# Macaron layer with an S4D mixing: float32 products of the output layer in one group of four banks per batch, and of the kernel's taps for four steps at a time

## The chip, the cores and the metric

One Trainium2 chip; the program runs on one of its cores. The metric is the device time of one execution in microseconds (us), as a median over runs. The engines are named as in the profile: PE (TensorE, the matrix products; PEld are its weight loads), DVE (VectorE), ACT (ScalarE), POOL (GpSimd), SP (the queue that issues most of the transfers).

## The reference, cut to what matters

B = 4 batches of L = 1024 tokens, D = 256 channels, HID = 1024, all float32:

```python
def ffn(x, w1, s1, w2, s2, h1, t1, h2, t2, w3, s3):
    h = silu((x @ w1.T) * s1) * ((x @ w2.T) * s2)     # 256 -> 1024
    h = gelu((h @ h1.T) * t1)                         # 1024 -> 1024
    h = gelu((h @ h2.T) * t2)                         # 1024 -> 1024
    return (h @ w3.T) * s3                            # 1024 -> 256

def mixing(x, ...):                                   # S4D
    K = 2 * einsum('dn,dnl->dl', C, exp(dtA[:, :, None] * t)).real   # taps, [D, L]
    y = irfft(rfft(x.T, 2 * L) * rfft(K, 2 * L), 2 * L)[:, :, :L]
    return gelu(y.T) @ W.T + b                        # W: the output layer, 256 -> 256

x = x + 0.5 * ffn(layernorm(x), ...)
x = x + mixing(layernorm(x), ...)
return x + 0.5 * ffn(layernorm(x), ...)
```

The matrices w1, w2, h1, h2 and w3 hold only -1, 0 and 1. The second `ffn` uses the same weights as the first.

## The kernel before, in words

**The FFN blocks.** The 4096 tokens are eight blocks of 512. The first FFN runs over f0 to f7, the second over g0 to g7. f0 to f7, g0 and g1 are single blocks (`ffn`, L374); g2 to g7 are three pairs of blocks whose two 1024 x 1024 layers use a Winograd scheme with 7 products in place of 8 (`ffn_pair`, L416). In a single block, `linear` (L362, matmuls at L366) makes one output tile of 128 x 512 in one PSUM bank: for each 128 rows of input a product with the high part of the activation and one with its low part, in a reduced float32 format that the profile calls fp32r. ACT applies the activation and copies the high part (`g`, L399; `h_f`, L401), DVE makes the low part by subtraction (`low_part`, L309). The products of w1 and w2 are `pa` and `pb`, those of h1 and h2 `p2` and `p3` (both are `p_f` or `p_g` in the profile, which leaves numbers out), those of w3 `po` (L617).

**The mixing.** It is an FFT convolution cut into matrix products, and these take true float32 operands; each such matmul is two records in the trace. Four kinds of them: `pk` (L883) makes the taps from the modes, once for the whole program; `pf` (L956) is the forward transform of the taps (`pf_k`) and of each batch (`pf_m`); `pi` (L1134) is the inverse transform; `pw` (L1159) is the output layer. All the rest of the mixing, complex products with `kr` and `ki` and butterflies (`y`, `z`, `p`, `q`, `u`, `v`, `w`), is element work on DVE through one helper (L155).

**How the two are laid together.** The mixing is written as generators. `all_aside` (L1221) runs the taps (`kernel_steps`), their transform (`kernel_spectrum`), then `mix(b)` for the four batches, each as soon as its two f blocks are done. In an `ffn` block, each of the 16 output tiles of h1 and h2 calls `tick` (L1245) after its own work has been written out, and `tick` advances the generator until an allowance of DVE work is used up (`STEP_WORK` 3600, 3400 once f7 is done; only operations on DVE count, not matmuls or ACT's copies) or until the generator yields `PAUSE`. So a `PAUSE` puts at least one output tile of FFN products between what is ahead of it and what is behind it. After a `PAUSE` with allowance left, in the later blocks, up to two steps of fillers may run: sums of weights for the pairs (`weight_sums`, stored to DRAM) and a check of the weights (`weight_checks`). `ahead` (L1279) moves the preparation of the next block on: load, norm, squares and a turn through DRAM (`sq`, `moved`, `xf`) and the split into parts (`parted`: `xt`, L356 and L309). A scheduler then fixes the order of each engine's list; each engine takes its list in order.

**Taps.** `kernel_steps` runs over two groups of channels; the first falls into block f1, the second into f2. In each, eight steps make a tile `p` on DVE (three operations, with `po`) and append it to `ready`. `products` makes eight `pk` matmuls from one step, 128 x 64 weights and 32 columns; two steps fill a bank, and eight ACT copies (L895, 64 x 64) then take that bank to the `taps` tiles.

**Output layer.** In `mix`, the inverse's result goes through the gelu to `yt`. Then, for j in steps of two, `xr` (128 x 512, part of x1) is loaded by SP, a bank `pw` takes four matmuls from `yt` and `wt_sb`, DVE adds the bias (`yw`), POOL adds `xr` (L1175), and a store to x2 (L1176) follows.

**Buffers.** All banks of PSUM, eight of 128 x 512, are one ring (`ps`). `half` (L167) is one ring of 19 tiles of 128 x 512 in SBUF, for nearly everything of the mixing and for `g`; `ring` (L171) is one of 15 for the activations in two parts. A tile of a ring waits for the last user of the tile that had its place before.

Of the kernel before, what the change touches and what calls it, by code (L numbers as in the profile page):

```python
# [21 lines left out]
J = L // P  # L22
# [86 lines left out]
def macaron_layers(  # L109
# [54 lines left out]
    def bank(name):  # L164
        return psum.tile([P, 512], F32, tag="ps", name=name)

    def half(name, *shape, dtype=F32):  # L167

        return work.tile([P, *(shape or (512,))], dtype, tag="half", name=name, bufs=19)
# [35 lines left out]
    def column(i):  # L205
        return cst_sb[:, i : i + 1]

    def positions(t, b, j, n=2):
        return t[b].rearrange("(p j) d -> p j d", j=J)[:, j : j + n, :]
# [599 lines left out]
    def powers(d0, first, n, name):  # L809


        ch = 512 // n
        at = cst_sb[:, None, first : first + n].to_broadcast([P, ch, n])

        def of(i):
            return adt[:, i, d0 : d0 + ch, None].to_broadcast([P, ch, n])

        a, k, e = (half(f"{t}_{name}", ch, n) for t in ("a", "k", "e"))
        tt(e, of(0), at, ALU.mult)
        nc.scalar.activation(e, e, AF.Exp)  # L820
        tt(a, of(1), at, ALU.mult)
        reduce_angle(a, a, k)
        yield
        c = k
        sin_cos(c, a)
        yield
        tt(c, c, e, ALU.mult)
        tt(a, a, e, ALU.mult)
        yield c, a
# [3 lines left out]
    def kernel_steps():  # L833


        yield from kernel_factors()
        taps.extend(half(f"taps_{i}", 2, 2, DD) for i in range(J // 2))
        n = 512 // NA
        group = 512 // A1
        shape = [P, n, A1, A0]  # L840
        for g0 in range(0, DD, group):

            for got in powers(g0, C_A1, A1, f"1_{g0}"):
                yield
            c, i = got
            to_re, to_im = half(f"to_re_{g0}", group, A1), half(f"to_im_{g0}", group, A1)
            ts(to_re, c, column(C_RE), None, ALU.mult)
            stt(to_re, i, column(C_IM), to_re, ALU.mult, ALU.add)
            ts(to_im, c, column(C_IM), None, ALU.mult)
            stt(to_im, i, column(C_MINUS_RE), to_im, ALU.mult, ALU.add)  # L850
            yield
            for fine in powers(g0, C_A0, A0, f"0_{g0}"):
                yield

            qd = []
            some = 512 // NB
            for d0 in range(g0, g0 + group, some):
                for got in powers(d0, C_B, NB, f"b_{d0}"):
                    yield
                c, i = got  # L860
                for t, m in ((c, 0), (i, 1)):
                    by = c_dt[:, m, d0 : d0 + some, None].to_broadcast([P, some, NB])
                    tt(t, t, by, ALU.mult)
                for d1 in range(0, some, per_tile):
                    t = half(f"qd_{d0 + d1}", per_tile, 2, NB)
                    nc.gpsimd.memset(t, 0.0)
                    qd.append(t)
                    for h in range(2):
                        part, ch = slice(h * 64, (h + 1) * 64), slice(d1, d1 + per_tile)
                        tt(t[part, :, h, :], c[part, ch], i[part, ch], ALU.add)  # L870
                yield

            pk = None
            ready = []

            def products(d1, a):

                nonlocal pk
                at = d1 % per_tile
                if at == 0:  # L880
                    pk = psum.tile([P, per_tile, 2, NB], F32, tag="ps", name=f"pk_{g0 + d1}")
                for i in range(n):
                    nc.tensor.matmul(  # L883
                        pk[0:NA, at + i, :, :].rearrange("p h b -> p (h b)"),
                        a[:, i].rearrange("p a b -> p (a b)"),
                        qd[d1 // per_tile][:, at + i, :, :].rearrange("p h b -> p (h b)"),
                        start=True,
                        stop=True,
                    )
                if at + n == per_tile:  # L890
                    first = g0 + d1 + n - per_tile
                    for i, t in enumerate(taps):
                        for over in range(NB // J):
                            b0 = over * J + 2 * i
                            nc.scalar.copy(  # L895
                                t[over * NA : (over + 1) * NA, :, :, first : first + per_tile],
                                pk[0:NA, :, :, b0 : b0 + 2].rearrange("p d h b -> p b h d"),
                            )

            for d1 in range(0, group, n):  # L900
                re, im = fine

                def outer(coarse, t):
                    return (
                        coarse[:, d1 : d1 + n, :, None].to_broadcast(shape),
                        t[:, d1 : d1 + n, None, :].to_broadcast(shape),
                    )

                a, o = (half(f"{t}_{g0 + d1}", n, A1, A0) for t in ("p", "po"))
                tt(a, *outer(to_re, re), ALU.mult)  # L910
                tt(o, *outer(to_im, im), ALU.mult)
                tt(a, a, o, ALU.add)
                ready.append((d1, a))
                if len(ready) == 4:
                    for old in ready[0:2]:
                        products(*old)
                    del ready[0:2]
                yield
            yield PAUSE
            for old in ready:  # L920
                products(*old)
            yield
# [113 lines left out]
    def mix(b, xn):  # L1036
# [108 lines left out]
        todo = []  # L1145
        for j in range(0, J, 2):
            xr = half(f"xr_{b}_{j}", 2, D)
            nc.sync.dma_start(xr, positions(x1, b, j))
            todo.append((j, xr))
            if len(todo) == 1:  # L1150
                continue
            yield PAUSE
            results = []
            for j, xr in todo:
                ps = bank(f"pw_{b}_{j}")
                results.append(ps)
                for e in range(2):
                    for dc in range(DC):
                        nc.tensor.matmul(  # L1159
                            ps[:, e * D : (e + 1) * D],  # L1160
                            yts[dc][j // JQ][:, (j % JQ + e) * P : (j % JQ + e + 1) * P],
                            wt_sb[:, dc, :],
                            start=(dc == 0),
                            stop=(dc == DC - 1),
                        )
            yield PAUSE
            for (j, xr), ps in zip(todo, results):
                y = half(f"yw_{b}_{j}", 2, D)
                tt(
                    y,  # L1170
                    ps.rearrange("p (e d) -> p e d", e=2),
                    bias_sb[:, None, :].to_broadcast([P, 2, D]),
                    ALU.add,
                )
                nc.gpsimd.tensor_tensor(y, xr, y, ALU.add)  # L1175
                stores.dma_start(positions(x2, b, j), y)  # L1176
            todo = []
# [43 lines left out]
    def all_aside():  # L1221


        yield from kernel_steps()
        yield from kernel_spectrum()
        xn = None
        for b in range(B):
            while ("f", 2 * b + 1) not in done:
                yield PAUSE
            if xn is None:  # L1230
                xn = [load_half(x1, b, g) for g in range(2)]
                yield PAUSE
            yield from mix(b, xn)
            xn = None
            done.append(("m", b))
# [150 lines left out]
```

## Time and profile before

| | before |
|---|---|
| median of 3 runs | 1368.81 us (1368.12 to 1369.08) |
| profiled execution, its own time | 1368.22 us |
| span from its first to its last instruction | 1366.4 us |
| clock granted to PE, mean | 0.999 of full speed |
| PE busy with matmuls / weight loads | 1351.8 us (99%) / 1125.2 us (82%) |
| DVE, ACT, POOL busy | 74%, 57%, 22% |
| `pk` (taps): 256 records | 16.4 us busy, 223 ns each, from 111.9 to 225.7 us |
| `pw` (output layer): 128 records | 28.9 us busy, 379 ns each, from 403.0 to 900.7 us |

How to read it: a matmul's busy time includes the time it spends in the pipeline, so that neighbours overlap and the sum of busy times says more of how full PE is than of what one matmul costs. What a matmul costs is the distance from its start to the next one's. A wait is listed with the engine, the tile and the line that ended it. Times in a timeline are counted from the start of the span; equal neighbours are put together in one row, with their number (x8).

In the profile the `pk` records come in eight groups of 32: four in f1 (from 111.93, 117.76, 123.59 and 133.06 us) and four in f2 (202.75, 208.59, 218.05, 223.88). The `pw` records come in eight groups of 16: 403.0 and 413.7 (f4), 540.2 (f5), 576.3 (f6), 704.2 and 714.9 (f7), 886.8 and 897.5 (g1).

### The profile page before, as it was taken

The page shows a single profiled execution, that of the slowest core. Times are in us where ns is not written, and L with a number is a line of the kernel's source. Part 1 is how long each engine was busy: PE and PEld are TensorE (multiplying, and loading weights), DVE is VectorE, ACT ScalarE, POOL GpSimd, SP SyncE. Part 2 cuts the span into 40 slices and gives each one's busy share as a digit, 9 for nine tenths or more (in the row PEclk, how much of TensorE's full clock was granted, in tenths as well). Part 3 has the DMA queues.
Part 4 walks back from the last instruction along what each step waited for, and adds up shares of the span by engine and source line. Part 5 has one row for each costly group of instructions (what it writes and reads, how often), then busy time and mean ns, then how long its engine had stood idle before and what let it go on. Part 6 is the DMA issues. An engine that isn't in the chain of part 4 may idle for free.

```text
span 1366.4 us, 18201 instructions
## 1 busy us (share of the span) xinstructions
PE 1351.8 (99%) x6300; PEld 1125.2 (82%) x6300; DVE 1008.8 (74%) x1886; ACT 776.4 (57%) x1236; POOL 297.1 (22%) x454
## 2 busy tenths in 40 slices
PE   9999999999999999999999999999999999999997
PEld 7888878888888888887888887888888888888886
DVE  6997885749865887668855799658885778568654
ACT  5985966454444543534545745436776476656663
POOL 4440220421205213420214012052300430040002
PEclk9999999999999999999999999999999999999999
DMA  9440121414125236454054342352655145521441
GB/s 354 114 141 3 31 62 39 146 33 124 39 93 204 59 108 188 125 183 120 20 169 115 115 154 47 115 166 83 208 165 168 31 139 181 170 66 62 160 148 34
DMA packets 121670, 160.00 MB, mean 117 GB/s; under 512 B 73872, under 2 KB 84112, under 8 KB 116192
## 3 DMA queue, kind: packets, MB, share of 16 engines
q1 hardware_dynamic: 99296, 99.41, 23.8%
q0 software_dynamic: 22000, 59.07, 13.9%
q8 instruction: 51, 0.84, 0.3%
q14 instruction: 51, 0.42, 0.1%
q10 hardware_dynamic: 272, 0.26, 0.1%
HBM read 120.95 MB, written 37.75 MB: 116 GB/s over the span
## 4 chain that ended last, share of the span: by engine, by line
PE 50%; DVE 4%; issue 1%; DMA 0%; ACT 0%; SPq 0%; DVEq 0%; POOLq 0%; POOL 0%; ACTq 0%
PE p_g L366 7%; PE p3a_g L510 6%; PE p2a_g L510 6%; PE p2x_g L510 5%; PE p3x_g L510 5%; PE p_f L366 4%; PE pa_g L366 4%; PE pb_g L366 4%; PE po_g L617 3%; PE pi L1134 1%; PE pw L1159 1%; DVE y L155 1%; PE po_f L617 1%; PE po_g L648 1%; PE pa_f L366 1%; PE pb_f L366 1%
## 5 line engine op out<-in xcount | busy, mean ns | idle before, releaser
L366 PE MATMUL p_f<-ha_f,h_sb 128*128 128x512 f32 x1024 | 238.7, 392 | 0.1
L366 PE MATMUL p_f<-h_f,h_sb 128*128 128x512 f32 x1024 | 237.1, 391 | 0.0
L366 PEld LDWEIGHTS p_f<-h_f,h_sb 128*128 128x128 f32 x1024 | 192.1, 188 | 39.7
L366 PEld LDWEIGHTS p_f<-ha_f,h_sb 128*128 128x128 f32 x1024 | 191.4, 188 | 40.4 <-DVE ha_f L309 0.8
L399 ACT ACTIVATE g_f<-p_f,sc_sb 128x512 f32<-128x512 f32 x128 | 87.4, 689 | 210.2 <-PE p_f L366 178.6
L309 DVE TENSOR_TENSOR h_f<-g_f,h_f 128x512 fp32r<-128x512 f32 x128 | 88.1, 691 | 113.4 <-ACT h_f L401 113.2
L630 POOL TENSOR_TENSOR y_g<-xr_g,y_g 128x512 f32<-128x512 f32 x14 | 19.9, 1431 | 323.8 <-DVE y_g L629 310.1
L401 ACT CAST h_f<-g_f 128x512 fp32r<-128x512 f32 x128 | 78.4, 619 | 3.1
L524 ACT ACTIVATE h_g<-h_g,sc_sb 128x512 f32<-128x512 f32 x72 | 52.0, 724 | 43.9 <-DVE h_g L480 43.6
L339 POOL DMA_DIRECT2D moved<-sq_f x56 | 30.6, 554 | 197.8 <-DVE sq_f L155 197.8
L366 PE MATMUL pa_f<-xt_f,w_sb 128*128 128x512 f32 x256 | 70.5, 391 | 1.8 <-DVE xt_f L356 1.2
L339 POOL DMA_DIRECT2D moved<-sq_g x64 | 34.9, 552 | 167.5 <-DVE sq_g L155 166.3
L366 PE MATMUL pb_f<-xt_f,w_sb 128*128 128x512 f32 x256 | 70.0, 389 | 0.0
L366 PE MATMUL pa_g<-xt_g,w_sb 128*128 128x512 f32 x256 | 68.9, 389 | 0.0
L366 PE MATMUL pb_g<-xt_g,w_sb 128*128 128x512 f32 x256 | 68.9, 389 | 0.0
L617 PE MATMUL po_f<-h_f,w_sb 128*128 128x512 f32 x256 | 60.7, 391 | 1.6 <-ACT h_f L401 0.9
L385 DVE SCALAR_TENSOR_TENSOR g_f<-pb_f,sc_sb,g_f 128x512 f32<-128x512 f32 x64 | 46.6, 746 | 19.7 <-ACT g_f L384 10.0
L366 PE MATMUL p_g<-ha_g,h_sb 128*128 128x512 f32 x256 | 59.4, 391 | 0.1
L366 PE MATMUL p_g<-h_g,h_sb 128*128 128x512 f32 x256 | 59.3, 391 | 0.0
L366 PEld LDWEIGHTS pa_f<-xt_f,w_sb 128*128 128x128 f32 x256 | 48.0, 188 | 12.8 <-DVE xt_f L356 1.6
L617 PEld LDWEIGHTS po_f<-h_f,w_sb 128*128 128x128 f32 x256 | 47.6, 188 | 13.0 <-DVE h_f L309 2.0
L399 ACT ACTIVATE g_g<-p_g,sc_sb 128x512 f32<-128x512 f32 x32 | 22.1, 690 | 60.8 <-PE p_g L366 50.3
(302 smaller groups left out, 2887.9 us busy)
## 6 DMA issues: line engine op xcount, KB each, us to landing
w<-q SPq DMA_DIRECT2D x42, 1024.0 KB, 5.0
q<-s POOLq DMA_DIRECT2D x40, 256.0 KB, 4.4
h_sb<-in_h_dram POOLq DMA_DIRECT2D x8, 1024.0 KB, 14.4
given<-in_h_dram SPq DMA_DIRECT2D x32, 256.0 KB, 3.4
kr<-k_hat SPq DMA_DIRECT2D x20, 256.0 KB, 2.8
ki<-k_hat SPq DMA_DIRECT2D x20, 256.0 KB, 3.1
q<-h_sb POOLq DMA_DIRECT2D x16, 256.0 KB, 4.8
xr_f<-in_x_dram SPq DMA_DIRECT2D x64, 64.0 KB, 2.5
```

The source lines that it names most:

```text
L155: return op(dst, *args, **kwargs)
L309: return nc.vector.tensor_tensor(t[:, 1, :], src, t[:, 0, :].bitcast(F32), ALU.subtract)
L339: stores.dma_start(moved[k].rearrange("(c r) a q -> a r c q", r=SQ)[a], sq[a * SQ : (a + 1) * SQ].rearrange("r c j s -> r c (j s)"),)
L366: nc.tensor.matmul(ps, w[:, k, m * P : (m + 1) * P], acts[k][:, part, :], start=(k == 0 and part == 0), stop=(k == n - 1 and part == parts ...
L385: nc.vector.scalar_tensor_tensor(g if split else t[:, 0, :], pb, sc_sb[:, 1, m : m + 1], g, ALU.mult, ALU.mult)
L399: nc.scalar.activation(g, ps, AF.Gelu, scale=sc_sb[:, layer, m : m + 1])
L401: nc.scalar.copy(t[:, 0, :], g)
L510: nc.tensor.matmul(ps, weights[:, c, m * P : (m + 1) * P], ops[c][:, part, :], start=(first and c == 0 and part == 0), stop=(c == QK - 1 a ...
L524: nc.scalar.activation(o, src, AF.Gelu, scale=sc_sb[:, layer, m : m + 1])
L617: nc.tensor.matmul(ps, w3_sb[:, k, o * P : (o + 1) * P], acts[k][:, part, :], start=(k == order[0] and part == 0), stop=(k == order[-1] an ...
L630: nc.gpsimd.tensor_tensor(y, rest[k], y, ALU.add)
L648: nc.tensor.matmul(ps[:, e * D : (e + 1) * D], acts[k][:, part, (i + e) * P : (i + e + 1) * P], w3_sb[:, k, :], start=(k == 0 and part == ...
```

## The change

Two conditions are changed. In `kernel_steps` the products of the taps are held back until six steps are ready, then made for four of them; the other four are made at the end of the group of channels. Before, they were made for two steps whenever four were ready, and for the last two at the end. In `mix`, all four tiles `xr` of a batch (J is 8) are loaded first, then, after a `PAUSE`, all four banks of `pw` are filled in one go, and after one more `PAUSE` the four results are taken out. Before, this was done twice per batch with two banks each. So each batch has two `PAUSE`s fewer. What is computed stays the same.

```diff
@@ -911,10 +911,10 @@
                 tt(a, a, o, ALU.add)
                 ready.append((d1, a))
-                if len(ready) == 4:
-                    for old in ready[0:2]:
+                if len(ready) == 6:
+                    for old in ready[0:4]:
                         products(*old)
-                    del ready[0:2]
+                    del ready[0:4]
                 yield
             yield PAUSE
             for old in ready:
@@ -1147,7 +1147,7 @@
             xr = half(f"xr_{b}_{j}", 2, D)
             nc.sync.dma_start(xr, positions(x1, b, j))
             todo.append((j, xr))
-            if len(todo) == 1:
+            if len(todo) < J // 2:
                 continue
             yield PAUSE
             results = []
```

## The prediction

> **What bounds the kernel.** I read the page's busy row and slices first, then the waits of TensorE, then PE's list in time, and last the ACT and DVE lists just ahead of each wait. The busy row, and TensorE's waits (us in total, times, longest):
>
> ```profile
> PE 1351.8 (99%) x6300; PEld 1125.2 (82%) x6300; DVE 1008.8 (74%) x1886; ACT 776.4 (57%) x1236; POOL 297.1 (22%) x454
> PE warm L1266 <- POOL ident masks.py:199: 2.6, 1, 2.6
> PE pa_f L366 <- DVE xt_f L356: 1.2, 1, 1.2
> PE po_f L617 <- ACT h_f L401: 0.9, 1, 0.9
> PE po_f L617 <- DVE h_f L309: 0.7, 1, 0.7
> ```
>
> TensorE is the bound: outside the head it waits some 4 to 7 us in 1366. So the time is PE's own issue plus a handful of waits, all at ends of blocks, where DVE or ACT delivers a block's last activation or the next block's first input late. The change moves both terms.
>
> **PE's own issue.** The starts of successive matmuls in the trace are 226.7 ns apart for the FFN's fp32r products, 215.7 for a float32 record of `pf` or `pw`, 111.7 for `pi`, 58.1 for `pk`. A group of taps in the timeline (start, length, line, names, count):
>
> ```profile
> 122.60 1.07 PE L366 MATMUL p_f<-ha_f,h_sb 128*128 128x512 f32 x4
> 123.59 2.05 PE L883 MATMUL pk<-qd,p 128*64 128x32 f32 x32
> 125.58 0.96 PE L366 MATMUL p_f<-ha_f,h_sb 128*128 128x512 f32 x3
> ```
>
> From the last fp32r start before such a group to the eighth after it takes 4.020 us; 8 x 226.7 + 32 x 58.1 is 3.673. The rest, **0.347 us**, is the price of going into the group and out of it, the same for all eight groups of taps. The same sum for a `pw` group of 16 records gives 5.280 - 5.265 = **0.015 us**, for all eight of them.
>
> **The Trainium skill.** Perfetto Trace Analysis, "Identifying the Most-Contended Engine", says that matmul busy share is a poor measure and the share of weight loads better: 99% against 82% here, so I count starts, not busy time. PSUM — Partial Sum Buffer, "Engine vs sequencer instructions", says that ScalarE's and VectorE's queues are strictly first in, first out and matmuls keep program order; the trace agrees (the ACT and DVE lists below run back to back in the program's order), so a late operation delays all behind it. ScalarE: Activation LUTs, "What ACT_TABLE_LOAD costs", puts a load at about 1283 ns plus a drain of 1380. Here a load takes 1.28 us and the next operation starts 0.02 later, so I use 1.30. No page prices going between fp32r and float32.
>
> **The change part by part.** *Taps:* eight groups of 32 records become four of 64, two in f1 and two in f2; nothing is added. *Output layer:* eight `pw` groups of 16 become four of 32. Matmuls, copies, additions, loads and stores stay the same in number. Two pauses fewer per batch also let the planner take the mixing of batches 1 and 2 one or two ticks earlier; fillers (weight sums and checks) go later. The transfers: four `xr` loads per batch go out together on SP, four stores follow each other, and four `yw` additions (0.68 us each on DVE, 1.43 on POOL) come in a burst. Nothing waits for `yw` soon: POOL is 22% busy and x2 is read a block later. Four banks of eight are held instead of two; the next reuse is eight allocations on, when the bank is empty.
>
> 1. *Switches of f2:* two groups of taps less, 2 x 0.347 = -0.69 us. No table load stands near them in ACT's new order, so I count all of it. If the copies came late by a load (1.3), it would be +0.6 instead.
>
> 2. *f1:* the same -0.69 on PE. But ACT's order there changes. Before:
>
> ```profile
> 135.14 1.72 ACT L895 COPY taps<-pk 64x64 f32<-64x64 f32 x8 [0.65 <-PE pk L883]
> 136.88 1.28 ACT L820 ACT_TABLE_LOAD   x1
> 138.18 0.63 ACT L820 ACTIVATE e<-e 128x512 f32<-128x512 f32 x1
> 138.83 1.28 ACT L399 ACT_TABLE_LOAD   x1
> 140.12 0.69 ACT L399 ACTIVATE g_f<-p_f,sc_sb 128x512 f32<-128x512 f32 x1
> 140.83 1.28 ACT L740 ACT_TABLE_LOAD   x1
> 142.12 0.63 ACT L740 ACTIVATE a<-a 128x512 f32<-128x512 f32 x1
> ```
>
> In the changed order 16 taps copies, the exponential's table and `e`, and the sine's table and `a` stand together ahead of `g` of the tile before last, and one load more falls before the last two tiles. Added up with these durations from 132.6 us: 16 copies 3.46, loads Exp, Sin, Gelu 3.9, `e`, `a` and `g` 2.0, load Sin 1.3, `k` 0.73 give 144.0 for `k`, 144.7 for the last-but-one high part, 147.3 for the last. PE enters the h2 products at 141.73 (142.42 less 0.69) and wants that high part in its 13th product, at 144.45: a wait of 0.6 to 0.85 in all. What is late next: DVE is dense from 142.8 to 180 and ends f1. Before:
>
> ```profile
> 177.82 1.72 DVE L155 TENSOR_TENSOR qd<-k_b,a_b 64x256 f32<-64x256 f32 x4
> 179.56 0.69 DVE L309 TENSOR_TENSOR h_f<-g_f,h_f 128x512 fp32r<-128x512 f32 x1
> 178.86 0.73 PE L617 MATMUL po_f<-h_f,w_sb 128*128 128x512 f32 x2 [0.89 <-ACT h_f L401]
> 180.31 0.72 PE L617 MATMUL po_f<-h_f,w_sb 128*128 128x512 f32 x2 [0.72 <-DVE h_f L309]
> ```
>
> The last low part, 179.56 to 180.25, releases f1's last product. That DVE chain starts with work on `k`, which by the same adding up comes at 145.33 instead of 144.79, behind the low part of the last-but-one tile, so f1 ends **0.5 us later** than before, although PE has 0.69 less to do. If DVE made up the shift in its one idle gap of 0.7, f1 would gain: ends -0.69 and +0.9.
>
> 3. *`pw` groups and neighbours:* 4 x 0.015 = -0.06; in f7 the inverse products now stand together in place of two pieces, -0.03; f4's last wait of 0.1 goes, -0.1. Sum -0.19.
>
> 4. *f5, from h1 to h2:* the mixing's butterflies of batch 1 come a tick earlier. From the first h2 low part at 485.19 to the low part of the last tile DVE then has 43 operations, 26.4 us by their rows, so that part is ready at 512.35. PE wants it in its 20th product from 507.66, at 511.97: +0.4, and with a start of its own 0.05, **+0.45** (0 to 0.9). PE has no wait there before.
>
> 5. *End of f6.* Before, DVE and PE:
>
> ```profile
> 643.35 0.69 DVE L155 TENSOR_TENSOR z<-x_m,ki 128x512 f32<-128x512 f32 x1
> 644.07 0.69 DVE L155 TENSOR_TENSOR y<-y,z 128x512 f32<-128x512 f32 x1
> 644.67 0.76 DVE L356 CAST xt_f<-xf_f 128x512 fp32r<-128x512 f32 x2
> 645.15 0.50 PE L366 MATMUL pa_f<-xt_f,w_sb 128*128 128x512 f32 x1 [1.15 <-DVE xt_f L356]
> ```
>
> The input of f7 is behind batch 2's complex products. These start a tick or two earlier but more of them, about 20 at 0.60 each, now precede it, against fewer fillers. Adding up DVE's new list gives the first copy of `xt` at 645.5 instead of 644.67, PE resuming at 646.0 against 645.15. PE itself arrives 0.1 earlier. **+0.7** with rounding (-0.3 if the products start a full tick earlier, +1.7 if a load of `kr` or `ki` (2.8 and 3.1 us to land) comes late).
>
> 6. g0, g1 and the three pairs: PE's, DVE's and ACT's orders are those of before but for one tiny product and fillers, and PE waits nowhere in the pairs: 0.
>
> Sum: -0.69 + 0.5 - 0.19 + 0.45 + 0.7 = **+0.8 us** on the profiled execution of 1368.22 (span 1366.4, 1.8 around it), so 1369.0. That execution lies 0.6 below the median of the runs, 1368.81, so as a median **1369.6**. The difference that a measurement can tell is about 0.2%, 2.74 us.
>
> **Rivals.** *A. Only the switches count.* Waits keep their places and sizes, f1 included: 4 x -0.347 - 0.19 = -1.6, so 1367.2, within 0.2%. For it: the switches are fixed prices; against: ACT's and DVE's new orders in f1 and f6. *B. Earlier mixing clears the block ends.* If batch 2's products are done before `xt` of f7 is ready, the 1.15 at 645 goes, its neighbour of 0.3 too, and the 1.55 at the end of g0 shrinks because fillers left that stretch: -1.6 - 1.5 - 1.2 = -4.3, so 1364.5, faster. Against it: g0's DVE order is unchanged. *C. Slower: ring slots at f6.* The tiles of the mixing and of the weight sums share a ring of 19; in the new order four `xr` tiles at once take their turn, and some of batch 2's tiles follow a slot that a weight sum's store still holds. If such a store lands late DVE stops in the middle of the products, and `xt` of f7 waits behind them. PE already waits there, so each us of it is a us of the end; 4 us (a store's landing, 4.4 to 5.0 us in the page's list of transfers) on top of the +0.8 is 1373.6. It decides from 2 us of DVE standing still. *D. f1's chain:* the extra table load delays DVE's start by 1.3 in full and takes a second one with it in f1's next tiles, +2.6 in place of +0.5: 1371.7, slower by 0.21%.
>
> **Numbers.** Forecast 0.33 (own range 1368.0 to 1371.0), A 0.20, B 0.14, C 0.20, D 0.13. D lies on the limit: half counts as slower, and so does a tenth of the forecast; of A and the forecast a few hundredths fall to faster. Faster 0.20, same 0.48, slower 0.32. The range reaches from A's lower side into half of B (1365.2) to C's 1374.0.
>
> **What would show it.** Right: four groups of `pk` x64 with 0.35 each; a wait of PE in f1's first h2 products on `h_f` L401; f1's last product later by 0.5; a wait of `p_f` on DVE near 512; the wait on `xt_f` at f6's end nearer 2 us. Wrong: `xt_f` gone from the waits (B), the price of a group of 64 twice that of 32 (then nothing is saved), or DVE idle ahead of `y`, `z` with a DMA as releaser (C).

## The result, and the profile after

The changed kernel takes 1371.33 us in the median of 22 runs (1369.86 to 1373.12), against 1369.01 for the kernel before in the same comparison (22 runs, 1368.12 to 1370.60): 2.3 us more, ratio 1.0017 with an interval of 1.0011 to 1.0023. Run again beside the later experiments (19 runs) it gave 1.0018 (1.0011 to 1.0025). So it is slower, by an amount just within the 0.2% that the prediction took as its limit. The profiled execution took 1371.72 us (span 1369.9), 3.5 more than that of before.

The busy row of the page and TensorE's waits, after:

```profile
PE 1353.1 (99%) x6300; PEld 1125.5 (82%) x6300; DVE 1009.7 (74%) x1886; ACT 777.1 (57%) x1237; POOL 299.7 (22%) x454
PE pa_f L366 <- DVE xt_f L356: 1.6, 1, 1.6
PE po_f L617 <- DVE h_f L309: 1.4, 2, 0.7
PE po_f L617 <- ACT h_f L401: 1.3, 1, 1.3
PE p_bad L724 <- ACT g_g L399: 0.7, 1, 0.7
PE p_f L366 <- DVE h_f L309: 0.2, 1, 0.2
```

The work is the same but for one more instruction on ACT (1237 against 1236, the table load). The waits tell the rest: `xt_f` at f6's end 1.6 in place of 1.2, a second wait of `po_f` on DVE, 1.3 in place of 0.9 at f1's end, and two waits that were not there, of `p_bad` (g1) and of `p_f` (f5's h2 products).

I took the distance of each PE start to the next, less the plain distance of its kind (226.7 ns, 215.7, 111.7, 58.1, as in the prediction), and summed the excess by block and layer. Only the places that differ are shown, in us, from the profiled executions:

| place | before | after | taps alone (e1) | output layer alone (e2) |
|---|---|---|---|---|
| f1, h1 products (two groups of taps fewer) | 1.91 | 1.31 | 1.28 | 1.98 |
| f1, h2 products | 0.02 | 0.30 | 0.30 | 0.02 |
| f1's end | 2.16 | 2.61 | 2.61 | 2.17 |
| f2, first products | 0.03 | 1.63 | 0.01 | 0.04 |
| f2, h1 products (two groups fewer) | 1.22 | 0.54 | 0.53 | 1.22 |
| f4's end | 0.11 | 0.00 | 0.09 | 0.00 |
| f5, h2 products | 0.03 | 0.53 | 0.03 | 0.49 |
| f5's end | 0.00 | 0.98 | 0.00 | 1.00 |
| f6, and f7's start | 1.55 | 2.35 | 1.26 | 2.38 |
| g1, h2 products | -0.06 | 0.72 | -0.06 | 0.72 |

These differences add to 4.0 us; with the small ones left out here, PE's last start lies 3.83 later, and the span is 3.5 longer.

**A group of taps**, timeline of PE after:

```profile
114.51 1.07 PE L366 MATMUL p_f<-ha_f,h_sb 128*128 128x512 f32 x4
115.51 3.92 PE L883 MATMUL pk<-qd,p 128*64 128x32 f32 x64
119.36 0.96 PE L366 MATMUL p_f<-ha_f,h_sb 128*128 128x512 f32 x3
```

By the same sum as before (5.887 us from the last fp32r start to the eighth after, less 5.532) a group of 64 costs 0.355 against 0.347 for one of 32. The price belongs to the group, not to its records.

**f1's end and f2's start**, PE after, and then a row of the table of stretches (start:end, length, busy time of PE, PEld, DVE, ACT and POOL with their instructions, then PE's granted clock, DMA share, GB/s):

```profile
178.86 0.73 PE L617 MATMUL po_f<-h_f,w_sb 128*128 128x512 f32 x2 [1.34 <-ACT h_f L401]
180.30 0.73 PE L617 MATMUL po_f<-h_f,w_sb 128*128 128x512 f32 x2 [0.71 <-DVE h_f L309]
181.35 0.63 PE L366 MATMUL pa_f<-xt_f,w_sb 128*128 128x512 f32 x1
181.78 0.63 PE L366 MATMUL pb_f<-xt_f,w_sb 128*128 128x512 f32 x1
```
```profile
180.00:190.00 10.00, 9.70 (x36) 7.87 (x37) 6.64 (x12) 6.71 (x10) 6.56 (x9) 0.83 0.41 72
```

f1's last low part releases PE at 180.30; before it was 180.31. So f1 ends when it did, and the group prices saved in f1 became waiting time. Then the starts of eight products are 0.427 us apart in place of 0.227, with a granted clock of 0.50 from 182 to 184: 1.6 us that no wait shows.

**f5's end**: DVE, POOL and PE after. Before, DVE had nothing of the mixing in this stretch, and PE did not wait.

```profile
551.82 3.12 DVE L155 TENSOR_TENSOR s<-h_sb 128x512 f32<-128x512 f32 x2
554.86 0.80 DVE L356 CAST xt_f<-xf_f 128x512 fp32r<-128x512 f32 x2
555.59 0.67 DVE L309 TENSOR_TENSOR h_f<-g_f,h_f 128x512 fp32r<-128x512 f32 x1
```
```profile
551.39 3.00 POOL L1175 TENSOR_TENSOR yw<-xr,yw 128x512 f32<-128x512 f32 x2 [3.49 <-DVE yw L155]
```
```profile
556.31 0.96 PE L617 MATMUL po_f<-h_f,w_sb 128*128 128x512 f32 x3 [0.69 <-DVE h_f L309]
```

Two sums of weights take 3.12 us here; elsewhere two such take 1.28. They run while POOL adds `xr` to `yw`, and the last low part of f5, behind them in DVE's list, comes too late for PE.

**f6's end**, DVE after and PE after:

```profile
645.14 2.49 DVE L155 TENSOR_TENSOR u_i<-p_i,q_i 128x512 f32<-128x512 f32 x4
647.55 0.41 DVE L155 TENSOR_SCALAR x_g<-x_g,mv_g,rstd_g 128x256 f32<-128x256 f32 x1
647.87 0.75 DVE L356 CAST xt_f<-xf_f 128x512 fp32r<-128x512 f32 x2
```
```profile
648.34 0.50 PE L366 MATMUL pa_f<-xt_f,w_sb 128*128 128x512 f32 x1 [1.62 <-DVE xt_f L356]
```

Where `y` and `z` stood ahead of `xt` before, the later butterflies `p`, `q`, `u` of the same batch stand now: the mixing has come further, and the first input of f7 is 1.62 late in place of 1.15.

**g1**, DVE and PE after:

```profile
908.22 0.15 DVE L721 TENSOR_REDUCE total<-miss 128x1 f32<-128x44 f32 x1
```
```profile
908.51 0.19 PE L724 MATMUL p_bad<-ones,total 128*1 128x1 f32 x2 [0.72 <-ACT g_g L399]
```

`p_bad` sums the result of the weight check, and PE takes it in its order; before, it did not wait for it. The wait is put down to ACT, but its operand `total` is DVE's, done at 908.37, just ahead of its start.

### The profile page after: what moved, and what is told of

Read it like the earlier page. It is cut to its first block, busy times and chain, and to the rows that moved or that the text cites. A ratio compares the mean times of both kernels' runs of the same rounds, so it can differ in the third digit from the quotient of the medians.

```text
span 1369.9 us, 18228 instructions
## 1 busy us (share of the span) xinstructions
PE 1353.1 (99%) x6300; PEld 1125.5 (82%) x6300; DVE 1009.7 (74%) x1886; ACT 777.1 (57%) x1237; POOL 299.7 (22%) x454
## 4 chain that ended last, share of the span: by engine, by line
PE 87%; DVE 9%; issue 2%; POOL 1%; ACT 1%; DMA 0%; DVEq 0%; POOLq 0%; ACTq 0%
PE p_f L366 27%; PE p_g L366 7%; PE p2a_g L510 6%; PE p3a_g L510 6%; PE p2x_g L510 5%; PE p3x_g L510 5%; PE pa_f L366 4%; PE pb_f L366 4%; PE pa_g L366 4%; PE pb_g L366 4%; PE po_g L617 3%; PE po_f L617 3%; PE pi L1134 2%; PE pf_m L956 2%; DVE y L155 2%
## 5 line engine op out<-in xcount | busy, mean ns | idle before, releaser
L630 POOL TENSOR_TENSOR y_g<-xr_g,y_g 128x512 f32<-128x512 f32 x14 | 20.0, 1434 | 324.9 <-DVE y_g L629 324.9
L384 ACT ACTIVATE g_f<-pa_f,sc_sb 128x512 f32<-128x512 f32 x64 | 43.5, 688 | 24.5 <-PE pa_f L366 22.5
```

The costliest lines, as they stand in the source:

```text
L384: nc.scalar.activation(g, pa, AF.Silu, scale=sc_sb[:, 0, m : m + 1])
```

## The experiments

The times of the kernel before in the three comparisons below were 1368.99 (33 runs; e1 to e4), 1368.99 (57 runs; e5 to e8) and 1368.60 (39 runs; e9 to e12). A ratio stands with its interval of 95%; it need not be the quotient of the two medians.

### Each part alone (e1, e2)

e1 has only the first hunk of the change, e2 only the second.

> Only the taps in groups of four steps, the output layer as before. Theory 1 (two prices and the clock): f2 gains two group prices, -0.69 us; f1 comes out even, since its end hangs on DVE (-0.69 of group prices, +0.3 of a wait in its h2 products, +0.45 at its end); in the executions in which PE then waits a little longer at f1's end the first eight products of f2 run 0.20 us slower each, +1.6. So -0.7 without and +0.9 with the slow products, and no change after f2. Theory 2 (the group prices are all that the taps bring, the slow products belong to something else): -1.4 in every execution.

Measured: 1368.65 (13 runs), ratio 1.0002 (0.9993 to 1.0010). The trace has f1 even (1.28, 0.30 and 2.61 in the table, +0.10 in all) and f2 0.69 shorter, as expected. PE stands as long at f1's end as in the changed kernel, and yet f2's first products run at full speed in this execution.

> Only the output layer in one group of four banks, the taps as before. Theory 1 (two pauses fewer per batch move DVE's work of the next batch ahead of what PE waits for): a new wait of 0.5 us in f5's h2 products, one of 1.0 at f5's end, the wait at f6's end longer by 0.8, one of 0.8 at the tiny product of the weight check in g1, less 0.2 of group prices and of a wait in f4: +2.9 us, and the first products of f2 at full speed. Theory 2 (the slow products of f2 and the taps are most of the loss): under +1.

Measured: 1371.31 (13 runs), ratio 1.0017 (1.0008 to 1.0025), with all four waits in their places (table). The loss of the change is that of the output layer; the taps are worth nothing that the times can tell.

### One group, with the pauses put back (e3)

```diff
-            if len(todo) == 1:
+            if len(todo) < J // 2:
                 continue
...
                 stores.dma_start(positions(x2, b, j), y)
+                if j == 2:
+                    yield PAUSE
+                    yield PAUSE
```

> The output layer in one group of four banks, with two more pauses after the second result, so that the planner has as many pauses as before and the next batch starts where it did. Theory 1 (it is the planner's order, not the group): the waits at 512, at f5's end, at f6's end and in g1 are those of the kernel before, so -0.06 us from four group prices of 0.015, within 0.3 of it. Theory 3 (the group itself: four banks, four loads and four additions in a burst, four places of the ring of 19 at once): the waits stay, +2 to +3.

Measured: 1374.52 (5 runs), ratio 1.0045 (1.0031 to 1.0059). Theory 1 had foretold no change, so as a full account it fell. It was right on two waits: those at 512 and at f5's end are gone (0.03 and 0.00). f6's end is little better (1.77; 1.92 in e2, and 0.8 to 1.3 in the profiles of before, e1, e4, e7 and e12, which all have the old output layer), g1 is worse (2.38), and there are two new waits, 2.05 in f4 (0.4 of it ahead of a transform) and 1.21 at f7's end. In f4, DVE, POOL and PE of e3:

```profile
422.47 3.24 DVE L309 TENSOR_TENSOR h_f<-g_f,h_f 128x512 fp32r<-128x512 f32 x1 [1.19 <-ACT h_f L401]
```
```profile
422.62 2.53 POOL L1175 TENSOR_TENSOR yw<-xr,yw 128x512 f32<-128x512 f32 x2
```
```profile
425.77 1.45 PE L366 MATMUL p_f<-h_f,h_sb 128*128 128x512 f32 x5 [1.36 <-DVE h_f L309]
```

A low part that takes 0.69 elsewhere takes 3.24, to 425.71, POOL's two additions having ended at 425.15, and PE waits for just this one. At f7's end a weight check takes 3.15 us in the same way, at 727.21 beside POOL's additions at 727.26. The Trainium skill describes it (SBUF — State Buffer, "Who interferes with whom"): a VectorE instruction with two inputs in SBUF contends with a GpSimd instruction that reads SBUF, since they share a port that one of them holds. The times here agree with it; whether it is this port, no run here can tell. That gave theory 4.

### POOL's addition left out (e5, e6)

e5 is e2, and e6 is e3, each without this line, so that x2 lacks x1:

```diff
-                nc.gpsimd.tensor_tensor(y, xr, y, ALU.add)
                 stores.dma_start(positions(x2, b, j), y)
```

> The output layer in one group of four banks, taps as before, and POOL's addition of x1 to the output layer's result (L1175) left out, so that x2 lacks x1; all other lists of instructions stay in their order up to g1's end. Theory 4 (at f5's end DVE's two sums s, 3.1 us in place of 1.3, stand against POOL's additions of yw, which read SBUF at the same time): the sums take 1.3 us, the wait of 1.0 at f5's end is gone, the one of 0.5 in f5's h2 products stays, as do f6's end and the one in g1, which come of DVE's order: about 1.0 us less than e2, +1.3 over before. Theory 1 in its first form (all four waits come of DVE's order): as e2, +2.3.

Measured: 1370.87 (20 runs), ratio 1.0010 (1.0004 to 1.0017). f5's end, DVE of e5:

```profile
551.22 1.28 DVE L155 TENSOR_TENSOR s<-h_sb 128x512 f32<-128x512 f32 x2
552.42 0.76 DVE L356 CAST xt_f<-xf_f 128x512 fp32r<-128x512 f32 x2
553.11 0.67 DVE L309 TENSOR_TENSOR h_f<-g_f,h_f 128x512 fp32r<-128x512 f32 x1
```

The list is the same, the sums take 1.28, and f5's end costs 0.00 in place of 1.00. The other three waits stay: 0.67 in f5's h2 products, 1.93 at f6's end, 0.55 in g1. So the wait at f5's end comes of POOL's additions, and the others do not. The median fell by 0.4 us against e2, not by 1.0, and the intervals of the two overlap. In the profiled executions PE's list, from its first FFN product to its last start, is 1.0 shorter, as forecast (1351.57 against 1352.58). In the median a lower clock may hide the rest, as 11 of e5's 20 executions had a mean clock of 0.997 or below and 3 of e2's 13; that is not shown.

> The kernel of e3 (one group of four banks, with as many pauses as before), and POOL's addition of x1 (L1175) left out, so that x2 lacks x1. Theory 4: the waits that e3 brought, 2.0 us in f4, 1.2 at f7's end, 0.4 at f6's end and 2.4 in g1, are gone, since DVE's operations of 3.2 us take 0.7 again: within 0.4 us of the kernel before (-0.06 from the group prices). Theory 3 (four banks, four loads and four results at once hold PSUM or the ring of 19): the waits stay, +5.

Measured: 1371.28 (12 runs), ratio 1.0017 (1.0009 to 1.0026), 3.2 us less than e3. The low part at 422.67 takes 0.69; f4 and f7's end are back at 0.03 and 0.00, f6's end is at 0.82. The wait in g1 stays at 2.38, so the forecast, within 0.4 us of before, missed there. The reason is PE's order. Before, the second group of `pw`, 16 records and 3.45 us of starts, stood between g1's fourth h2 tile and `p_bad`, and `total` was made under it:

```profile
897.50 3.61 PE L1159 MATMUL pw<-wt_sb,yt 128*128 128x256 f32 x16
```

With all 32 records together two tiles earlier nothing stands there, and `total` is behind that tile's low part on DVE. In the changed kernel the cover is gone too; `p_bad` stands one tile later there, and waits 0.8.

e5 and e6 differ in the two pauses alone. With them (e6) the wait in f5's h2 products is 0.02 in place of 0.67 and f6's end 0.82 in place of 1.93, so these two come of the earlier start of the mixing. The wait in g1 does not: with the pauses it is longer.

### Versions that might beat both (e4, e7, e8)

e4 keeps f1 and the output layer as before and merges the taps in f2 alone:

```diff
-                if len(ready) == 4:
-                    for old in ready[0:2]:
+                held, made = (6, 4) if g0 else (4, 2)
+                if len(ready) == held:
+                    for old in ready[0:made]:
                         products(*old)
-                    del ready[0:2]
+                    del ready[0:made]
```

> Groups of four steps in the second group of channels (f2) alone, the first (f1) and the output layer as before. Theory 1: two group prices, -0.69 us, and nothing else moves, f1's end included. If the price of a group grew with its size, or ACT's copies came late in f2, it would be 0 or above.

Measured: 1368.19 (13 runs), 0.80 less than before, ratio 0.9993 (0.9985 to 1.0001). In the trace f2's h1 products have 0.53 for 1.22, -0.69, and f1's end is as it was (2.19 against 2.16).

e7 has `(9, 9)` in place of `(6, 4)`, so that all eight steps of f2 are made after the pause.

> In f2 all eight steps of the taps in one group of 128 records after the pause, f1 and the output layer as before. If a group's price does not grow with its size: three prices less, -1.04 us. If four banks in a row or sixteen tiles p held make ACT or DVE late in f2, there are new waits in f2 and it is 0 or above.

Measured: 1368.93 (13 runs), ratio 0.9999 (0.9991 to 1.0008). The scheduler put one FFN product into the group: 112 records, one product, 16 records. The two pieces cost 0.69 together, as e4's two groups do. The forecast of -1.04 counted on a third price saved, and that did not come; nothing else was lost in the trace.

e8 has e7's taps, e3's output layer, and the addition of `xr` on DVE.

> A version with all the parts that should pay: f2's taps in one group (-1.04), the output layer in one group with as many pauses as before (-0.06), and the addition of x1 on DVE in place of POOL, 16 operations of some 0.65 us. Theory 4: nothing stands against DVE any more and PE's waits are those of e6, so about -1.0. If the additions' own 10 us of DVE fall ahead of what PE waits for at a block's end, each shows there as 0.65 to 2.6 us, and it is above the kernel before.

Measured: 1372.12 (21 runs), ratio 1.0020 (1.0013 to 1.0026): slower, where -1.0 was the forecast. PE waits 0.79 in f4 (in part for the load of `m_m`, 0.5), f6's end is at 1.58, g1 at 2.36, for want of the cover as in e6.

### The half-speed products (e9, e10, e11, e12)

The Trainium skill (TensorE: Matmul & The Clock Gate, "What's actually happening") says that PE's clock is halved after an idle window of some 3.4 us and given back after a busy one of that length. The eight slow starts, 0.427 each, make 3.4 us, which agrees; but PE had stood only 1.34 and 0.71 us, with two products between. In e10 DVE's chain that ends f1 was lengthened:

```diff
                     nc.scalar.copy(t[:, 0, :], g)
+                    if name == "f1" and layer == 3 and m == 4:
+                        for _ in range(3):
+                            low_part(t, g)
                     low_part(t, g)
```

and in e9, in `last_squares`, PE was given something to do there:

```diff
+                if split and name == "f1" and o == DC - 1 and k == order[-2]:
+                    idle = bank("idle")
+                    for _ in range(5):
+                        nc.tensor.matmul(
+                            idle, w3_sb[:, k, 0:P], acts[k][:, 1, :], start=True, stop=True
+                        )
```

> The changed kernel, with five matmuls of no use (their bank is read by nobody) placed at f1's end, where PE stands 1.5 us for the last high part, and cover 1.1 of it. No wait of another engine is shortened. If the half-speed products after f1's end follow from PE standing still there: mean granted clocks of 0.997 and below, which 9 of 22 executions of the changed kernel showed, come about as seldom as in the kernel before (16 of 90), and the median is 0.2 to 0.4 us below that of the changed kernel run beside it. If the clock has nothing to do with that wait: the same share and the same median.

> The changed kernel, with DVE's low part of f1's fifth h2 tile made four times in place of once (the same values), three operations of 0.6 us more in the chain that ends f1. PE stands some 1.8 us longer at f1's end. If the half-speed products follow from PE standing still: they come in nearly all executions, about 1.8 + 0.6 x 1.6 = 2.8 us above the changed kernel's median, mean clock 0.997 or below. If not: +1.8 and the clocks as they were.

> The changed kernel itself, as the measure for the two above: 2.3 us over the kernel before, about four executions in ten at a mean clock of 0.997 or below, and in a profile with a clock of 0.999 no half-speed products at f2's start.

Measured: e11, the changed kernel, 1371.08 (19 runs); e10 1374.17 (5 runs, ratio 1.0039, 1.0025 to 1.0053), 3.1 above it; e9 1371.49 (13 runs, ratio 1.0020, 1.0012 to 1.0028), 0.4 above it. The same row of the table of stretches, from e10:

```profile
180.00:190.00 10.00, 8.51 (x27) 6.62 (x27) 6.17 (x12) 4.38 (x6) 5.20 (x6) 0.66 0.38 67
```

e10 was right: f1's end has 4.56 for 2.66, the first products of f2 have 2.05 of excess, and all five executions have a mean clock of 0.997 or below. e11 was right on the median and on the share (7 of 19); its profile has a clock of 0.997 and the slow products in the same place as the first one (1.58). e9 was not: its own trace has no slow products, but 7 of 13 executions have a mean clock of 0.997, so the share did not fall. It also has a new 0.5 in f4, where a transform waits for its matrix. So standing longer at f1's end brings the half speed; whether standing less takes it away is not shown. Where the low clocks of executions without a trace lie is not known. Nor does 0.997 find them all: the mean takes in the half clock after PE's last product, 1.9 to 4.9 us long in the 14 traces, so an execution at 0.998 can hold such a stretch too.

The traces show why the same stands do not always bring it. In each of them the granted clock changes only at whole multiples of 3.413 us from its first change to full (174.08 us, where it halves in the changed kernel, are 51 of them), and that first change lies anywhere from 5.7 to 8.8 us after the span's start. Two such windows of the changed kernel, and one of e1:

```profile
177.87:181.28 3.41, 1.71 (x6) 1.14 (x7) 3.34 (x9) 1.34 (x3) 0.00 (x0) 1.00 0.52 82
181.29:184.70 3.41, 3.41 (x9) 2.68 (x9) 2.05 (x4) 2.75 (x4) 1.57 (x2) 0.50 0.46 72
```
```profile
178.80:182.20 3.40, 2.51 (x10) 1.77 (x11) 3.36 (x8) 1.29 (x3) 0.00 (x0) 1.00 0.69 109
```

Count as PE's work in a window its starts by their plain distances (in the first row 1.32 us of 3.41, since busy time takes in the pipeline). The windows that half clock follows hold 0.39 of work (changed kernel), 0.25 (e11), 0.27 and, already at half clock, 0.28 (e10), and at the programs' ends 0.20 or less. From f0 on, no window of the 14 traces with 0.41 or more is followed by it. In e1 the same two stands of PE fall on either side of a boundary, the windows hold 0.62 each, and the clock stays full. So in these traces it was not the length of one stand that decided, but how much of a window was idle, and that depends on where the windows lie in an execution.

As an estimate, one can lay such windows at every position over a trace, from f0 on, and ask in which share of the positions one of them holds 0.39 or less: 0.21 before (low mean clocks: 22 of 129 executions), 0.41 in e1 (5 of 13), 0.57 in the changed kernel (16 of 41), all in e10 (5 of 5), none in e12 (0 of 13). e5 (0.32, 11 of 20) and e9 (0.15, 7 of 13) have clearly more than that, so it is not the whole account. It also shows what e9 left open: its f1 no longer has such a window, but at f6's end one can hold as little as 0.36, as in the changed kernel. No kept trace has half clock there.

> Taps of f2 in two groups (e4), the output layer and f1's taps as before, and the five matmuls of no use at f1's end. Two group prices less, -0.7; if PE's stand at f1's end is what brings the lower clock in some executions of the kernel before too, 0.2 us more, and fewer clocks of 0.997 and below than in the kernel before.

Measured: 1368.16 (13 runs) against 1368.60, ratio 0.9994 (0.9986 to 1.0003). No execution had a clock of 0.997 or below, against 6 of 39 of the kernel before; that is too few to tell. In its profile f2 is 0.68 and f1's end 1.1 shorter, the latter being the covered wait and no gain in time, and two waits came in that belong to late transfers: 0.7 in f5's h2 products, after DVE had stood 1.92 for `ki`, and 0.5 in f4 for `m_m`. Neither e4 nor e12 is faster than the kernel before beyond its interval.

## Why the prediction was right and wrong

In all, +0.8 us was foretold and 2.3 measured: just above the forecast's own range (1371.33 against 1371.0), within the wide one that the rivals set, and at 0.17% just within the limit of 0.2%, which the interval crosses. That it stayed within is in part luck, since 1.8 us of it are costs that the sum had at nothing. The nearest number was D's, 1371.7, whose mechanism did not come. By its steps, in the profiled executions:

1. *Switches of f2*: -0.69 foretold, -0.68 measured.
2. *f1*: +0.5 foretold, +0.1 measured. The first half of the mechanism was right: one more table load, ACT later, a wait in the h2 products, f1's end set by DVE. Two terms were too large. The two high parts are ready at 144.31 and 146.96, not at 144.7 and 147.3, so the wait is 0.30 in place of 0.6 to 0.85. And DVE's shift, 0.26 (`to_re` at 145.05 in place of 144.79) where 0.54 was foretold, does not reach f1's end: its last low part starts at 179.56 in both kernels. The gap of 0.7 that the prediction named is not what took it up, for it stands in both lists, 0.70 from 160.94. DVE's lists meet again at 157.38: an operation on `k_b` runs from 155.98 for 1.36 before, from 156.63 for 0.71 after, and ends at 157.34 in both. What held it until then is not known; POOL writes to `qd` at that time (L866).
3. *`pw` groups and neighbours*: the eight groups of 0.015 became four of 0.018, and f4's wait of 0.1 went.
4. *f5, from h1 to h2*: +0.45 foretold, +0.50 measured; e3, with the old number of pauses, has none of it.
5. *End of f6*: +0.7 foretold, +0.8 measured with f7's start. With the old output layer this sum is 1.0 to 1.6 in five profiles, so that the size is sure to some 0.5 only.
6. What failed is the sentence "Nothing waits for `yw` soon", with the zero set for the burst, and step 6, which put "one tiny product and fillers" at 0. The question was not who waits for `yw`, but what stands beside it. At f5's end DVE's sums stand against POOL's additions, +1.0 (e5 takes it away). And the merging took from `p_bad` the group of products under which its operand was made, +0.8 in g1. The later fillers are not to blame for it: in e3 and e6, with the pauses back, the same product waits 2.4.

The profile before already had a sign of the first. A low part takes 2.52 there, against 0.69 elsewhere, beside POOL's addition of `xr_f` to `y_f` (L630, from 370.20 for 1.30):

```profile
369.55 2.52 DVE L309 TENSOR_TENSOR ha_f<-g_f,ha_f 128x512 fp32r<-128x512 f32 x1
```

Steps 1 to 5 add to about +0.6 and the two in step 6 to +1.8; less 0.1 in the small places that the table leaves out, that is the 2.3 that the medians show. The table's remaining 1.6 is the half-speed stretch, which the profile of before does not have. A lower mean clock is found in some executions of both kernels: 0.997 or below was seen in 16 of 41 of the changed kernel and in 22 of 129 of the one before. The executions with it are 1.2 us longer in the first comparison (1372.0 against 1370.8), so the share accounts for some 0.3 us of the difference, as an estimate.

Of the rivals, A (only the switches) and B (block ends cleared) fell with f5, f6 and g1. C (DVE stopped by places of the ring that stores hold) did not come: ahead of `xt` of f7 DVE does not stand still. Where DVE was held up, at f5's end and in e3, it was by POOL's additions: without them (e5, e6) those waits go, though the same tiles are held. D (f1's chain, +2.6) did not come. Of the signs named for being right, the groups at 0.35, the wait near 512 and the longer one on `xt_f` (1.62) came, and f1's last product 0.5 later did not.

Three small readings in the prediction are off: its parts of slower add to 0.30 and not 0.32, the 0.015 can be read from seven of the eight `pw` groups (`p_bad` follows the last one), and of C's 4.4 to 5.0 us for a store the 5.0 belongs to a load (`w<-q`).

## What to carry to other kernels

An operation that is given to POOL to spare DVE is not free: find which DVE operations with two SBUF inputs will stand beside it, and whether PE waits for the one behind them. Where a generator with an allowance shares out the work, taking away a pause is a change of schedule for everything after it, fillers included, and a cover, such as 3.45 us of products over a small result, can be worth more than the 0.015 that merging saves. A price per group, here 0.35 us for products of 32 columns, is real, but it is only gained where PE sets the end of the stretch, as in f2 and not in f1.

## What the runs showed that I had not expected

DVE's low part, 0.69 us alone, took 3.24 across two back-to-back additions of POOL, although by the profile it started 0.15 us ahead of the first: it did not get between them. And PE's clock can drop to half for 3.4 us after stands of only 1.34 and 0.71 us, in some executions and not in others, in these traces by where the windows of 3.413 us lay; with stands of 2.07 and 1.49 (e10) the mean clock was low in all five.
